# Toeplitz matrices fetched by half and copied on chip, and the experts' ends moved two steps behind their products, in a sequence mixer followed by a two-expert layer

## The chip, the cores and the metric

The kernel runs on one core of one Trainium2 chip. The metric is the device time of one execution in microseconds. Beside it stand the span and the trace of one profiled execution, from its first to its last instruction. The engines are TensorE (PE; its weight loads are PEld), VectorE (DVE), ScalarE (ACT), GpSimd (POOL) and SyncE (SP), and 16 DMA engines serve them all. SP issues ordinary transfers, POOL the indirect ones (gathers and scatters whose rows come from a table of indices).

## The reference

The input x has 2 sequences of 4096 tokens with 512 channels (8192 rows). After a layer normalisation, every channel is convolved causally with a kernel of its own, a sum of 16 decaying exponentials; and every token goes through its two best of 8 experts, 512x512 matrices, whose results are weighted and summed. The mixer's output times the silu of the experts' output is added to x.

```python
xn = _layernorm(x, axis=-1)
# mixer: q = 1 - sigmoid(delta) * sigmoid(alpha)
k = einsum('dnl,dn->dl', p * beta * exp(t * log(q)), gamma * scale)
s = irfft(rfft(xn^T) * rfft(k))[..., :l]^T + xn * omega
# experts
gate_logits = xf @ Wg.T + bg
topk_vals, topk_idx = jax.lax.top_k(gate_logits, 2)
gate_w = softmax(topk_vals)
all_out = einsum('nd,ehd->neh', xf, We) + be
g = silu(sum over the two of all_out[expert] * gate_w)
out = x + s * g
```

## The kernel before, in words

**Order of work.** All instructions of an engine are chained in the order in which the program names them (class InOrder): nothing is reordered on an engine, so an instruction that waits holds all that follow it there. Between engines only data and buffers set the order.

**Start (0 to 103 us).** 16 blocks of 4 chunks of x are loaded, normalised into `xn` (regions 0 to 3 of the buffer `big`, a quarter of the channels in each), transposed and multiplied with the gate's weights. The convolution kernels go to DRAM as `k_dram`.

**Mixer (103 to 326 us).** The 512 channels are 64 groups `g` of 8, four groups make one of 16 units `u`. A unit has products of the chunks' states (`states`, then two scans on VectorE), products with powers (`from_states`), and for each group 32 products with Toeplitz matrices (`from_chunks`), all summed in the banks `pys`; `outputs_end` copies them out, three banks by ScalarE and one by VectorE. A Toeplitz matrix of 64x64 is needed in both halves of the partitions, since `from_chunks` works with rows 0 to 63 for one half of the tokens and 64 to 127 for the other. `load_toep(g)` fetches the same 128 KB twice, once into each half of one of TB = 6 buffers, and is called five groups ahead. Between the groups the program lays other work by a table (`at(n, f, ...)`): the routing (two best experts, counting, index tables, with `val` made by POOL and consumed by TensorE), stores of the mixer's output to `s_dram` (64 of 256 KB), loads of the expert weights (16 of 512 KB, from group 33) and biases (8 of 256 KB, from group 56), and the first gathers of rows at group 58.

**Experts (326 us to the end).** The tokens are sorted by expert into NT = 71 tiles of 128 rows; round r = 0 does each token's first expert, round r = 1 its second, so `work_list` has 142 items. An item i passes through:

- `fetch(i)`: POOL gathers its rows of x (in round 1 only for the first FIRST = AHEAD + 1 tiles) and, in round 1, its rows of the mixer's output with weights and statistics from `s_dram`; AHEAD steps ahead.
- `fetch_first(i)`, in round 1: POOL gathers the first expert's result and x from `yx_dram`, which round 0 wrote.
- `mean_of(i)` (round 0) and `normalise(i)`: VectorE and a square root on ScalarE make the normalised rows, three steps ahead. `turn(i)`: TensorE transposes them and ScalarE copies them out of PSUM, two steps ahead.
- `expert(i)`: eight recorded products, whose weights are chosen by a register.
- the end, one step after: in round 0 `end_first` (VectorE adds the bias, POOL scatters into `yx_dram`); in round 1 `take_first` (ScalarE), `add_bias` and `add_expert` (VectorE, then silu on ScalarE), `put_out` (two VectorE steps, then POOL scatters to the output).

All this stands in one loop over i, whose body names the calls in a fixed order; the gathers of a step come ahead of its scatter on POOL, and the end of the earlier item comes ahead of the next `normalise` on VectorE. The products are held in a pool of 4 banks (`ps_e`), the transposes in one of 2 (`ps_t2`).

Of the kernel before, what the change touches and what calls it, by code (L numbers as in the profile page):

```python
# [8 lines left out]
FP = mybir.dt.float32  # L9
# [7 lines left out]
P = 128  # L17
EPS = 1e-5
SX = 4
IL = 2  # L20
AHEAD = 6
EARLY = 2
NOWHERE = float(1 << 20)

# [32 lines left out]
def tile_ssm_then_moe(  # L57
# [231 lines left out]
    with ExitStack() as ab:  # L289
# [33 lines left out]
        tri = abc.tile([P, P], BF)  # L323
        ones = abc.tile([P, P], BF)

        def load_toep(g):

            toep = toep_b[:, g % TB].rearrange("p h t -> p (h t)")
            src = k_dram[g * GD // IL : (g + 1) * GD // IL, 0:H]
            for h in range(2):  # L330
                io.sync.dma_start(
                    out=toep[h * H : (h + 1) * H].rearrange("p (h t) -> p h t", h=GD // IL),
                    in_=bass.AP(
                        src.tensor, src.offset, [[IL, H], [2 * H * IL, GD // IL], [1, H * IL]]
                    ),
                )
            return toep.rearrange("p (h t i) -> p h i t", i=IL, t=H)

        def powers_of(u):

# [92 lines left out]
        with ExitStack() as ph0:  # L433
# [180 lines left out]
            def gate_end(q):  # L614
                lt = ps_y.tile([P, LC, 32], FP, tag="py", name="lt")
                io.tensor.transpose(lt.rearrange("p c j -> p (c j)"), lqs_of.pop(q), ident)
                io.vector.tensor_add(
                    logits[:, q * LC : (q + 1) * LC, :], lt[:, :, 0:NE],
                    bc(gate_b.unsqueeze(1), P, LC, NE),
                )  # L620
# [61 lines left out]
                    )  # L682
            for i in range(LC):
                turn_chunk(NQ - 1, i)
            states(0, w.pop(0))
            for n in range(2):
                scan(n, decay.pop((0, n)))
# [2 lines left out]
            pys0 = banks()  # L690
            from_chunks(0, 0, pys0, toeps.pop(0))
            toeps[TB - 1] = load_toep(TB - 1)
            gate_end(NQ - 2)
            gate(NQ - 1)
            from_chunks(0, 1, pys0, toeps.pop(1))
            toeps[TB] = load_toep(TB)
            gate_end(NQ - 1)


# [251 lines left out]
        for u in range(NU):  # L951
            pys = banks() if u else pys0

            late = 0 if u else 1
            for i in range(2 * late, NS):
                g = u * NS + i
                if g + TB - 1 < G:
                    toeps[g + TB - 1] = load_toep(g + TB - 1)
                if i == 1 + late:
                    from_states(u, pys, powers.pop(u))  # L960
                    if u + 2 < NU:
                        powers[u + 2] = powers_of(u + 2)
# [12 lines left out]
                from_chunks(u, i, pys, toeps.pop(g))  # L975
                for f, args in todo:
                    if f not in first_of_group:
                        f(*args)
            outputs_end(u, sq_of(u * NS // GQ), pys)
# [4 lines left out]
    with ExitStack() as cc:  # L984
        mp = cc.enter_context(tc.tile_pool(name="more", bufs=1))
        ps_t = cc.enter_context(tc.tile_pool(name="ps_t2", bufs=2, space=PSUM))
        ps_e = cc.enter_context(tc.tile_pool(name="ps_e", bufs=4, space=PSUM))

        def more(n, width, name):
            return [mp.tile([P, width], FP, name=f"{name}{i}") for i in range(n)]  # L990

        xn_b += more(1, D, "xn")
        xnT_b += more(2, D, "xnT")
# [10 lines left out]
        for i in range(EARLY, 3):  # L1004
            mean_of(i)
            normalise(i)
            if i < 2:
                turn(i, ps_t.tile([P, KD, P], FP, name="pt"))
        held = None
        for i in range(n + 1):  # L1010
            r = work_list[i][0] if i < n else 1
            ended = work_list[i - 1][0] if i else None
            if i + AHEAD < n:
                fetch(i + AHEAD)
            if i + 3 < NT:
                mean_of(i + 3)
            if ended == 0:
                end_first(i - 1, held)
            if i == NT:
                for ii in range(NT, NT + AHEAD + 1):  # L1020
                    fetch_first(ii)
            elif i > NT and i + AHEAD < n:
                fetch_first(i + AHEAD)
            if ended == 1:
                add_expert(i - 1, held)
            if i + 3 < n:
                normalise(i + 3)
            if i + 2 < n:
                turn(i + 2, ps_t.tile([P, KD, P], FP, name="pt"))
            if i < n:  # L1030
                pe = ps_e.tile([P, D], FP, tag="pe", name="pe")
                expert(i, pe)
            if i >= NT:
                if i == NT:
                    take_first(i)
                if i < n:
                    add_bias(i)
                if i + 1 < n:
                    take_first(i + 1)
            if ended == 1:  # L1040
                put_out(i - 1)
            held = pe


# [45 lines left out]
```

## Time and profile before

| | us |
|---|---|
| median of 3 runs (943.41 to 953.67) | 945.86 |
| the profiled execution, its time | 945.91 |
| its span | 944.2 |
| busy in the span: PE / DVE / POOL / ACT | 813.7 / 583.1 / 499.4 / 365.0 |
| first expert product starts at | 325.84 |
| first gather from yx_dram starts at | 609.81 |
| last scatter starts at | 938.74 |
| DMA: 189.36 MB, of it by POOL's queue / by SP's | 126.79 MB / 61.38 MB |

A busy TensorE is not TensorE at its peak: products are pipelined and their ends are modelled. All instructions carry line 53 (a helper issues them), so they are told apart by the names of their tiles: `pe` are expert products, `pt` transposes, `py` the mixer's products, `toep_b` the Toeplitz buffers. A line of a timeline has start, duration, engine, operation, output and input tiles, and in brackets how long the engine had been idle before and what released it; a line of the chain of waits has start, duration and what the end was waiting for at that time. A line of waits has who waited for whom, total, times and longest.

### The profile page before, as it was taken

How to read it: one execution, taken by the hardware profiler on the slowest of the kernel's cores; microseconds unless marked ns; L12 is line 12 of the kernel's file. 1: busy time of each engine (PE TensorE's matmuls, PEld its weight loads, DVE VectorE, ACT ScalarE, POOL GpSimd, SP SyncE). 2: the span in 40 equal slices, each digit the busy share in tenths (PEclk: the TensorE clock that was granted, in tenths of full speed). 3: DMA queues.
4: the chain of work that ended last, by engine and by line, in shares of the span. 5: the costliest groups of instructions: out<-in, count | busy, mean ns of one | idle time of the engine just before them, and what ended most of it. 6: DMA issues, size and time to landing. Idle time of an engine off the chain costs nothing.

```text
span 944.2 us, 18704 instructions
## 1 busy us (share of the span) xinstructions
PE 813.7 (86%) x7035; PEld 482.2 (51%) x7038; DVE 583.1 (62%) x1147; ACT 365.0 (39%) x667; POOL 499.4 (53%) x480
## 2 busy tenths in 40 slices
PE   4989868887786599999999999888788996996996
PEld 3777657676675344445444444444343443443442
DVE  7786587567764255555555554185665675765685
ACT  6786645553652222222222222152332343433352
POOL 6776103220334055555555556677566675675672
PEclk9999878899997599999999999989898999997998
DMA  4667225989999995555555557588666876785771
GB/s 152 225 207 212 53 58 43 193 179 250 251 229 237 319 284 205 187 192 202 190 201 207 180 194 231 154 283 254 198 204 210 247 223 192 226 258 190 242 220 42
DMA packets 130151, 189.36 MB, mean 201 GB/s; under 512 B 19918, under 2 KB 85838, under 8 KB 130064
## 3 DMA queue, kind: packets, MB, share of 16 engines
q0 software_dynamic: 38048, 126.79, 41.0%
q1 hardware_dynamic: 92016, 61.38, 26.4%
q8 instruction: 58, 0.95, 0.4%
q14 instruction: 29, 0.24, 0.1%
HBM read 120.62 MB, written 73.01 MB: 205 GB/s over the span
## 4 chain that ended last, share of the span: by engine, by line
PE 61%; DVE 12%; issue 8%; DMA 8%; another core or an unknown queue 4%; POOL 4%; ACT 3%; SPq 1%; POOLq 0%; DVEq 0%; ACTq 0%
PE pe L53 43%; PE pt L53 7%; PE py L53 5%; DVE big L53 4%; DVE came_b L53 3%; PE ph L53 2%; DMA big<-in_x_rev 2%; ACT big L53 2%; DVE st L53 1%; PE lq L53 1%; DMA toep_b<-k_dram 1%; DMA big<-in_b_e 1%; POOL big L53 1%; DMA big<-yx_dram,x_idx 1%
## 5 line engine op out<-in xcount | busy, mean ns | idle before, releaser
L53 PE MATMUL pe<-big 128*128 x576 | 265.2, 604 | 0.8 <-DMA big<-in_w_e 0.8
L53 PE MATMUL pe<-big,xnT 128*128 x560 | 258.3, 605 | 0.0
L53 PEld LDWEIGHTS pe<-big 128*128 128x128 f32 x576 | 106.7, 195 | 109.2 <-issue 109.2
L53 PEld LDWEIGHTS pe<-big,xnT 128*128 128x128 f32 x560 | 103.6, 195 | 104.7 <-issue 104.7
L53 ACT ACTIVATE big<-big 128x512 f32<-128x512 f32 x103 | 66.6, 651 | 186.0 <-DVE big L53 117.9
L53 PEld LDWEIGHTS pt<-ident,big 128*128 128x128 f32 x636 | 88.9, 190 | 89.8 <-issue 78.4
L53 PE MATMUL pt<-ident,big 128*128 128x128 f32 x636 | 103.8, 301 | 34.8 <-DVE big L53 20.1
L53 POOL TENSOR_TENSOR val<-hot,token 128x568 bf16<-128x568 bf16 x32 | 38.9, 1214 | 157.5 <-DVE hot L53 130.6
L53 ACT COPY big<-pt 128x512 f32<-128x512 f32 x136 | 76.6, 593 | 99.3 <-PE pt L53 84.3
L53 PE MATMUL py<-big,toep_b 64*64 64x64 f32 x2048 | 88.5, 242 | 27.3 <-DMA toep_b<-k_dram 10.6
L53 POOL DMA_INDIRECT out<-big,o_idx x71 | 75.3, 1061 | 68.9 <-DVE big L53 49.7
L53 PEld LDWEIGHTS py<-big,toep_b 64*64 64x64 f32 x2048 | 77.8, 152 | 38.7 <-issue 14.5
L53 POOL DMA_INDIRECT yx_dram<-big,o_idx x47 | 57.9, 1231 | 72.1 <-DVE sm L53 68.0
L53 DVE TENSOR_TENSOR big<-pe,big 128x512 f32<-128x512 f32 x47 | 32.5, 691 | 88.3 <-PE pe L53 81.3
L53 ACT COPY xnT<-pt 128x512 f32<-128x512 f32 x70 | 40.5, 578 | 83.1 <-PE pt L53 73.4
L53 POOL TENSOR_SCALAR big<-big,stats 128x512 f32<-128x512 f32 x44 | 55.9, 1347 | 23.1 <-ACT stats L53 10.1
L53 DVE SCALAR_TENSOR_TENSOR big<-pe,sg,big 128x512 f32<-128x512 f32 x42 | 31.5, 750 | 53.1 <-PE pe L53 28.3
L53 POOL DMA_INDIRECT big<-in_x,x_idx x52 | 51.2, 984 | 20.2 <-issue 16.3
L53 ACT ACTIVATE sm<-sm,eps 128x1 f32<-128x1 f32 x71 | 20.9, 294 | 86.2 <-DVE sm L53 86.2
L53 POOL DMA_INDIRECT sg<-s_dram,x_idx x42 | 46.4, 1104 | 12.8 <-issue 9.8
L53 DVE TENSOR_TENSOR big<-big 128x512 f32<-128x512 f32 x73 | 50.3, 689 | 3.4 <-ACT big L53 1.9
L53 POOL DMA_INDIRECT big<-yx_dram,x_idx x44 | 44.3, 1007 | 14.9 <-issue 12.8
(152 smaller groups left out, 1089.2 us busy)
## 6 DMA issues: line engine op xcount, KB each, us to landing
big<-in_x_rev SPq DMA_DIRECT2D x16, 1024.0 KB
toep_b<-k_dram SPq DMA_DIRECT2D x128, 128.0 KB
s_dram<-big SPq DMA_DIRECT2D x64, 256.0 KB
big<-in_w_e SPq DMA_DIRECT2D x16, 512.0 KB
big<-in_b_e SPq DMA_DIRECT2D x8, 256.0 KB
out<-big,o_idx POOLq DMA_INDIRECT x71
big<-in_x,x_idx POOLq DMA_INDIRECT x52
yx_dram<-big,o_idx POOLq DMA_INDIRECT x47
```

What stands on the lines that cost most here:

```text
L53: return lambda *args, **kwargs: self.order.follow(make(*args, **kwargs))
```

## The change

First, `load_toep(g)` fetches one half only (rows 0 to 63 for even g, 64 to 127 for odd), and `double_toep(g)` copies it to the other half: ScalarE for groups with g % 4 of 0 or 2, POOL for the others. The copy stands two groups ahead of its use, after `from_chunks` of group g - 2.

Second, in the experts' loop the end of an item comes BEHIND = 2 steps after its product (1 at the very end), rows are made ready up to READY = 5 steps ahead and turned three ahead, AHEAD is 7 (so FIRST is 8), and the pools grow: `ps_e` has 6 banks, `xn` 4 buffers for 3, `xnT` 5 for 4, `x_b` 8 for 7. At the boundary of the rounds three gathers from `yx_dram` are named at once and the other five singly, one a step beside the regular one, where all seven stood together.

```diff
+DOUBLED = 2
+TO_ACT = (0, 2)
-AHEAD = 6
+AHEAD = 7
+READY = 5
+TURNED = 3
+BEHIND = 2
...
+        def toep_of(g, half):
+            return toep_b[half * H : (half + 1) * H, g % TB].rearrange("p h t -> p (h t)")
...
         def load_toep(g):
-            toep = toep_b[:, g % TB].rearrange("p h t -> p (h t)")
             src = k_dram[g * GD // IL : (g + 1) * GD // IL, 0:H]
-            for h in range(2):
-                io.sync.dma_start(
-                    out=toep[h * H : (h + 1) * H].rearrange("p (h t) -> p h t", h=GD // IL),
...
+            io.sync.dma_start(
+                out=toep_of(g, g % 2).rearrange("p (h t) -> p h t", h=GD // IL),
...
+        def double_toep(g):
+            copy = io.scalar.copy if g % NS in TO_ACT else io.gpsimd.tensor_copy
+            copy(toep_of(g, 1 - g % 2), toep_of(g, g % 2))
...
                 from_chunks(u, i, pys, toeps.pop(g))
+                if g + DOUBLED < G:
+                    double_toep(g + DOUBLED)
...
-        ps_e = cc.enter_context(tc.tile_pool(name="ps_e", bufs=4, space=PSUM))
+        ps_e = cc.enter_context(tc.tile_pool(name="ps_e", bufs=6, space=PSUM))
...
-            if i + 3 < NT:
-                mean_of(i + 3)
-            if ended == 0:
-                end_first(i - 1, held)
...
+            to_be = i + 3 + min((i + 1) // 2, READY - 3)
+            make_ready(to_be, True)
+            ends = range(ended, i - (BEHIND if i < n - 2 else 1) + 1)
+            ended = max(ended, ends.stop)
+            for e in ends:
+                if e < NT:
+                    end_first(e, held.pop(e))
+                elif e == ends[0]:
+                    add_expert(e, held.pop(e))
+            if ended >= NT:
+                for ii in late[: 3 if len(late) > AHEAD else 1]:
+                    late.remove(ii)
                     fetch_first(ii)
-            elif i > NT and i + AHEAD < n:
-                fetch_first(i + AHEAD)
...
+                if i + AHEAD < n:
+                    fetch_first(i + AHEAD)
+            make_ready(to_be, False)
+            for ii in range(turned, min(i + 2 + (i >= 4), n - 1) + 1):
+                turn(ii, ps_t.tile([P, KD, P], FP, name="pt"))
+                turned = ii + 1
             if i < n:
-                pe = ps_e.tile([P, D], FP, tag="pe", name="pe")
-                expert(i, pe)
...
+                held[i] = ps_e.tile([P, D], FP, tag="pe", name="pe")
+                expert(i, held[i])
+            if ended == NT and ends:
+                take_first(NT)
+                add_bias(NT)
+                take_first(NT + 1)
+            for e in ends:
+                if e >= NT:
+                    if e > ends[0]:
+                        add_expert(e, held.pop(e))
+                    if e + 1 < n:
+                        add_bias(e + 1)
+                    if e + 2 < n:
+                        take_first(e + 2)
+                    put_out(e)
```

More of the change, by code (lines that the diff above doesn't have):

```diff
@@ L324, in tile_ssm_then_moe @@
         ones = abc.tile([P, P], BF)
+        def toep_of(g, half):
+            return toep_b[half * H : (half + 1) * H, g % TB].rearrange("p h t -> p (h t)")
         def load_toep(g):
-            toep = toep_b[:, g % TB].rearrange("p h t -> p (h t)")
             src = k_dram[g * GD // IL : (g + 1) * GD // IL, 0:H]
-            for h in range(2):
-                io.sync.dma_start(
-                    out=toep[h * H : (h + 1) * H].rearrange("p (h t) -> p h t", h=GD // IL),
[L333 to L337, printed above, removed]
+            io.sync.dma_start(
+                out=toep_of(g, g % 2).rearrange("p (h t) -> p h t", h=GD // IL),
+                in_=bass.AP(
+                    src.tensor, src.offset, [[IL, H], [2 * H * IL, GD // IL], [1, H * IL]]
+                ),
+            )
+            return toep_b[:, g % TB].rearrange("p h t -> p (h t)").rearrange(
+                "p (h t i) -> p h i t", i=IL, t=H
+            )
+        def double_toep(g):
+            copy = io.scalar.copy if g % NS in TO_ACT else io.gpsimd.tensor_copy
+            copy(toep_of(g, 1 - g % 2), toep_of(g, g % 2))
         def powers_of(u):
@@ L684, in tile_ssm_then_moe @@
                 turn_chunk(NQ - 1, i)
+            for g in range(DOUBLED):
+                double_toep(g)
             states(0, w.pop(0))
@@ L692, in tile_ssm_then_moe @@
             toeps[TB - 1] = load_toep(TB - 1)
+            double_toep(DOUBLED)
             gate_end(NQ - 2)
@@ L696, in tile_ssm_then_moe @@
             toeps[TB] = load_toep(TB)
+            double_toep(DOUBLED + 1)
             gate_end(NQ - 1)
@@ L986, in tile_ssm_then_moe @@
         ps_t = cc.enter_context(tc.tile_pool(name="ps_t2", bufs=2, space=PSUM))
-        ps_e = cc.enter_context(tc.tile_pool(name="ps_e", bufs=4, space=PSUM))
+        ps_e = cc.enter_context(tc.tile_pool(name="ps_e", bufs=6, space=PSUM))
         def more(n, width, name):
             return [mp.tile([P, width], FP, name=f"{name}{i}") for i in range(n)]
-        xn_b += more(1, D, "xn")
-        xnT_b += more(2, D, "xnT")
+        xn_b += more(2, D, "xn")
+        xnT_b += more(3, D, "xnT")
         yx_b += more(4, 2 * D, "yx")
@@ L1003, in tile_ssm_then_moe, with make_ready @@
             fetch(i)
[L1004 to L1009, printed above, removed]
+        ready, turned, ended, held = EARLY, EARLY, 0, {}
+        def make_ready(upto, before_ends):
+            nonlocal ready
+            for i in range(ready, min(upto, n - 1) + 1):
+                if before_ends:
+                    if i < NT:
+                        mean_of(i)
+                else:
+                    normalise(i)
+                    ready = i + 1
@@ L1010, in tile_ssm_then_moe @@
+        late = list(range(NT, NT + AHEAD + 1))
+        for before_ends in (True, False):
+            make_ready(2, before_ends)
         for i in range(n + 1):
-            r = work_list[i][0] if i < n else 1
-            ended = work_list[i - 1][0] if i else None
             if i + AHEAD < n:
                 fetch(i + AHEAD)
-            if i + 3 < NT:
-                mean_of(i + 3)
-            if ended == 0:
-                end_first(i - 1, held)
-            if i == NT:
-                for ii in range(NT, NT + AHEAD + 1):
-                    fetch_first(ii)
-            elif i > NT and i + AHEAD < n:
-                fetch_first(i + AHEAD)
@@ L1024, in tile_ssm_then_moe @@
[L1024 to L1029, printed above, removed]
-            if i < n:
-                pe = ps_e.tile([P, D], FP, tag="pe", name="pe")
-                expert(i, pe)
[L1033 to L1039, printed above, removed]
@@ L1040, in tile_ssm_then_moe @@
-            if ended == 1:
-                put_out(i - 1)
-            held = pe
+            to_be = i + 3 + min((i + 1) // 2, READY - 3)
[10 more added lines that the diff above has]
+                    late.remove(ii)
+                    fetch_first(ii)
+                if i + AHEAD < n:
+                    fetch_first(i + AHEAD)
```

## The prediction

> **What bounds the kernel now.** I read the table by stage first, then the chain of waits around each place where TensorE loses busy time, then the timelines of POOL, VectorE and TensorE there.
>
> ```profile
> core 0: us, PE busy (x) PEld busy (x) DVE busy (x) ACT busy (x) POOL busy (x), PEclk, DMA share, GB/s
> 165.00:215.00 50.00, 40.81 (x1119) 34.80 (x1116) 29.57 (x45) 26.82 (x52) 11.77 (x11) 0.88 0.89 188
> 215.00:265.00 50.00, 39.54 (x1097) 34.00 (x1097) 36.23 (x64) 25.90 (x49) 9.71 (x8) 0.90 0.99 249
> 265.00:306.00 41.00, 29.24 (x788) 24.87 (x784) 24.50 (x40) 15.90 (x25) 17.00 (x15) 0.88 1.06 230
> 306.00:326.00 20.00, 8.02 (x77) 6.60 (x78) 5.73 (x15) 5.07 (x9) 0.95 (x1) 0.50 1.03 339
> 326.00:590.00 264.00, 264.00 (x810) 130.04 (x811) 139.92 (x335) 58.42 (x134) 150.93 (x137) 0.99 0.61 207
> 618.00:936.00 318.00, 280.82 (x818) 135.38 (x816) 217.94 (x345) 120.63 (x208) 210.98 (x199) 0.95 0.69 218
> ```
>
> Three regimes are seen. From 165 to 326 us (the sequence mixer) the DMA engines are full (share 0.89 to 1.06). From 326 to 590 us (the first round of experts) TensorE is busy all the time, 3.873 us for an item. From 618 to 936 us (the second round) no engine is full: 318 us for what would be 275 us (71 x 3.873).
>
> ```profile
> 293.39 5.44 DMA toep_b<-k_dram
> ...
> 305.22 10.78 DMA big<-in_b_e
> ...
> 316.01 9.59 DMA big<-in_w_e
> ...
> 325.84 6.00 PE pe L53 x8
> 314.72 0.47 PE L53 MATMUL py<-big,toep_b 64*64 64x64 f32 x2 [5.13 <-DMA toep_b<-k_dram]
> ```
>
> The end of the mixer hangs on transfers: the last Toeplitz groups, then biases and expert weights that queue behind them. The first expert product starts at 325.84 us.
>
> ```profile
> 658.51 0.98 POOL L53 DMA_INDIRECT yx<-yx_dram,x_idx  x1 [0.30 <-issue]
> 659.79 1.01 POOL L53 DMA_INDIRECT out<-big,o_idx  x1 [0.30 <-issue]
> 661.11 0.98 POOL L53 DMA_INDIRECT sg<-s_dram,x_idx  x1 [0.30 <-issue]
> 662.39 0.95 POOL L53 DMA_INDIRECT big<-yx_dram,x_idx  x1 [0.30 <-issue]
> 669.57 1.01 POOL L53 DMA_INDIRECT out<-big,o_idx  x1 [6.23 <-DVE big L53]
> 666.10 0.75 DVE L53 SCALAR_TENSOR_TENSOR big<-pe,big 128x512 f32<-128x512 f32 x1 [7.44 <-remote]
> 667.45 1.09 PE L53 MATMUL pt<-ident,big 128*128 128x128 f32 x4 [6.58 <-DVE big L53]
> DVE big L53 <- remote: 42.5, 8, 10.3
> ```
>
> The last line is from the waits of 618 to 936 us. VectorE stops for 5 to 10 us some eight times, TensorE then waits for rows that VectorE has not made, and POOL for a row to put out. But POOL is nearly full as well: each item costs it two gathers and a scatter. From 609.81 to 904.16 us I count 190 POOL starts; waits over the usual 0.3 us gap add up to 35.9 us, and the rest is 1.367 us a DMA, so 4.10 us an item when nothing holds it, against TensorE's 3.873. In the second round TensorE is not the resource to watch; POOL is.
>
> **What the Trainium skill says.** "Runtime: NRT & Kernel Launch", section Instruction fetch mechanics: each engine streams its program in blocks over its own DMA queue, the crossing mostly hidden. The page's own table has two instruction queues (58 packets, 0.95 MB; 29 packets, 0.24 MB, thus 8.3 KB each). VectorE's stops at 650, 718, 784 and 845 us are 61 to 68 us apart, some 16 or 17 items, so I read the "remote" stops as such fetches; in the first round all but one are hidden, in the second they are not. That the fetch is the cause is inferred. "DMA: Bandwidth & Descriptors", section Queues, rings and completion order: every DMA engine goes round-robin over the queues, a packet at a time; a fetch or a weight load then waits beside whatever else is queued. This fits, but no line shows it alone. "ScalarE: Activation LUTs", section What ACT_TABLE_LOAD costs: 186 ns + 0.833 ns an element with immediate operands, thus 613 ns for 512; the trace has 578 and 593 ns for its 128x512 copies.
>
> **Part 1: Toeplitz halves.** Removed: 64 of the 128 DMAs toep_b<-k_dram, 128 KB and 256 pieces of 512 bytes each. Price of a piece: in 165-215 us, 0.89 x 50 us x 16 engines = 712 us of engine time moved 9.4 MB, nearly all in 512-byte pieces, 18,400 of them: 39 ns. Some 41 of the removed DMAs lie after 165 us: 41 x 256 x 39 ns / 16 = 25.6 us of a stretch that is full from 165 to 326 us. That is the DMA side's bound: the weights could land by about 301 us. On SP 64 issues of 0.59 us go too, ahead of the stores, weights and biases in its order, and with them waits for earlier transfers.
>
> Then TensorE is late next. It ended group 61 at 302.1 us. Left are two groups at 1.97 us, eight transposes at 1.97 together and the transposes of one more item at 1.09: 309 us. Ahead of that stand 3.15 us in which TensorE waited for POOL's val, itself behind a gather that waited for stores (2.33 us), and 13.6 us of "issue" gaps between 165 and 300 us, where between 103 and 165 us (DMA share 0.38) there was under 1. Emptier queues should give back some; bounds 0 and 12 us, I take 4. So the first expert product starts at 305: 21 us earlier, bounds 12 and 26.
>
> Added: 32 copies of 64x512 on ScalarE at 0.58 (18.6 us in a stage where it is busy about half) and 32 on POOL. No such POOL copy is in the trace; its one-input TENSOR_SCALAR of 128x512 takes 1.35 us, which I take; a plain copy may be down at 0.8. That is 43 us on an engine with 46 us of work in 165-306 us. Both are issued two groups (some 6 us) ahead of use, so nothing of them is on TensorE's path unless the transfer is late. The new wait: a copy holds ScalarE or POOL until its half has landed. Behind it on ScalarE are the powers, the decays, w and the copies of py that free the banks; on POOL val and the first gathers. The load is issued five groups ahead and the copy waits for it after three, so about 9 us of lead where the products had 15. Only the last two groups overran 15 us before, with SP ten microseconds behind; with the queue relieved I cost it at 0, upper bound 5 us (included in the 12 above).
>
> **Part 2: experts.** First round: TensorE remains full, 3.873 us an item; end two steps later and rows earlier change only what waits beside it. Its 71 items are 275 us as before.
>
> Boundary: the second round's first gather from yx_dram has to wait for the last scatter of the first. Before, POOL had two gathers (1.29 + 1.26 us) ahead of that scatter; now FIRST is 8 and only one is left, and a part of its lag goes: first gather about 2.3 us earlier relative to TensorE. TensorE stood 6.0 us there; with rows turned three ahead it can run four items past the boundary, so that stall goes, but POOL sets the pace from here.
>
> Second round, POOL: from the first yx_dram gather to the last are 194 starts, 193 x 1.367 = 264 us plus waits. Of the 35.9 us of waits, about 14 follow TensorE's own short stops (at 693, 752, 818, 892 us): with TensorE up to three items ahead these are hidden. The VectorE stops remain, since add_expert, put_out and so the scatter all stand behind them. How much of a stop POOL can cover is set by a loop: scatter, two gathers, landing, normalise, add_bias, the two steps of put_out, next scatter. I measure it at one place: scatter at 640.00, yx_dram gather at 642.77, landed 647.67, output row done at 650.30: 10.3 us. Before, the loop spanned four items (4 x 4.10 = 16.4, so POOL could lag 6 us, and did: 5.6 us at 655.90). Now AHEAD is 7, but rows are taken five ahead and ended two behind: three items, 12.3 us, so a lag of 2.0 us only. Stops of 5.15, 7.4, 6.0, 6.0 and 10.3 us less 2 each are 25 us. Waits 36 to 25: 11 us gained. From the last gather to the end were 28.6 us (915.61 to 944.2), and I leave them.
>
> **Sum.** 21 + 2.3 + 11 = 34.3 us: span 909.9, and with 1.7 us around it (945.91 against 944.2) 911.6 us. The profiled execution is 0.05 us from the median of 945.86, so no shift.
>
> **Rivals.**
> 1. The stops are absorbed wholly, and only POOL's own work is left in round two: 609.8 - 23.3 = 586.5, + 264 + 28.6 = 879, so 881 us. For it: TensorE gets a cover of some 11 us. Against: every output row passes VectorE, then POOL, which cannot catch up at 4.10.
> 2. Stage one gains, but POOL waits as long as before in round two: 944.2 - 23.3, so 922.6 us. For it: the shorter loop; against: TensorE's stops were a third of its waits.
> 3. The mixer doesn't gain, because copies held by late transfers cost what the fewer bytes bring: 944.2 - 13.3, so 932.6 us. Against it: share 1.06 just where it ends.
> 4. Slower: the three-item loop. If a yx_dram gather takes longer than 4.9 us to land, the loop grows past 12.3 us and paces the round. There are some 20 trips (61 scatters / 3); each microsecond over 6.9 costs 20 us, so from 8.6 us of landing the whole gain is gone, and at 9.3 us the time is 911.6 + 48 = 960 us. For it: two transfers more are asked for early, and POOL idles less. Against: 4.3 to 5.2 us wherever the trace lets it be read, at a DMA share of 0.69.
>
> **How the numbers follow.** Forecast 911.6 us: 0.42. Rival 1: 0.16; rival 2: 0.18; rival 3: 0.12; rival 4: 0.12. The range of 882 to 937 takes in rival 1 to rival 3 and leaves out rival 4 and a little at the fast end. A measurement of this kernel tells about 1% from no change. Faster by over 1% (below 936.4): the forecast, rivals 1 and 2 and a quarter of rival 3, which ends near that bound: 0.79. Within 1%: 0.1. Slower: 0.11.
>
> **What would show it.** First expert product near 305 us, and no wait for toep_b in TensorE's last groups; ScalarE and POOL copies of toep_b without long waits for DMA. In the second round, POOL starts 1.37 us apart with waits of about 25 us, VectorE's remote stops still there, TensorE's waits at most short and spread. I am wrong if the first expert product starts after 315 us, if VectorE waits for yx_dram gathers at most steps (rival 4), or if POOL's spacing falls well under 1.36.

## The result, and the profile after

The changed kernel took 937.17 us (median of 17 runs, 930.88 to 942.35), the kernel before 946.03 us beside it (17 runs, 937.91 to 955.5): ratio 0.9908, 95% interval 0.9884 to 0.9931. It is faster by 0.9%, where 3.6% were forecast. The profiled execution has a span of 935.5 us, 8.7 less than before.

Two things have to be known for the numbers below. First, later sets of runs fell on different chips, and these are of two kinds: the kernel before takes some 947 us on some and some 900 us on others. Each set has the kernel before beside it, and ratios are taken within one set alone. Each of these chips was met in one set only, so a chip and its occasion cannot be told apart; "kind of chip" stands for both. Second, on chips of the second kind the kernel before falls into two groups (in one set 11 of 43 runs at 883 to 891 us, the others at 894 to 913), and the ratios rest mostly on the lower one, so there they stand above what the medians say.

The table by stage, with the columns of before:

```profile
core 0: us, PE busy (x) PEld busy (x) DVE busy (x) ACT busy (x) POOL busy (x), PEclk, DMA share, GB/s
165.00:215.00 50.00, 40.65 (x1148) 34.67 (x1145) 34.92 (x48) 35.27 (x67) 19.39 (x21) 0.95 0.70 168
215.00:265.00 50.00, 40.63 (x1183) 35.12 (x1189) 39.93 (x69) 34.11 (x61) 17.80 (x18) 0.95 0.87 220
265.00:306.00 41.00, 28.32 (x687) 24.16 (x673) 21.02 (x38) 14.50 (x24) 18.83 (x19) 0.83 1.00 285
326.00:590.00 264.00, 264.00 (x823) 130.50 (x822) 153.05 (x320) 51.77 (x130) 142.10 (x143) 1.00 0.59 205
618.00:936.00 318.00, 266.46 (x759) 126.93 (x757) 212.92 (x331) 114.21 (x196) 205.27 (x190) 0.93 0.64 206
```

The DMA engines did become emptier between 165 and 265 us (0.89 and 0.99 before), but TensorE's busy time there is the same as before within 1.1 us. Where the mixer ends, TensorE's timeline has:

```profile
294.71 0.63 PE L58 MATMUL tab<-val,at 128*128 128x142 bf16 x4 [6.30 <-POOL val L58]
295.27 3.68 PE L58 MATMUL py<-big,toep_b 64*64 64x64 f32 x58
310.83 1.09 PE L58 MATMUL pt<-ident,xn 128*128 128x128 f32 x4 [4.54 <-DVE xn L58]
312.64 1.19 PE L58 MATMUL pe<-big 128*128 x1 [0.73 <-DMA s_dram<-big]
```

and POOL's:

```profile
285.20 0.95 POOL L58 DMA_INDIRECT big<-in_x,x_idx  x1 [0.30 <-issue]
292.83 0.61 POOL L58 COPY toep_b<-toep_b 64x512 f32<-64x512 f32 x1 [6.69 <-DMA toep_b<-k_dram]
293.53 1.13 POOL L58 TENSOR_TENSOR val<-hot,token 128x568 bf16<-128x568 bf16 x1
```

TensorE's last long waits for a Toeplitz transfer are gone (5.13 us at 314.72 before). The same kind of late transfer now holds POOL's copy for 6.69 us, `val` stands behind the copy, and TensorE waits 6.30 us for `val`. The first expert product starts at 312.64 us instead of 325.84.

The second round, from TensorE's, VectorE's, ScalarE's and POOL's timelines around one stop, and from the table of waits of 618 to 936 us ("remote" stands where the signal that ended a wait has no instruction that ended shortly before it):

```profile
629.74 3.60 PE L58 MATMUL pe<-big 128*128 x8
636.11 0.63 PE L58 MATMUL pt<-ident,big 128*128 128x128 f32 x4 [2.77 <-ACT xnT L58]
636.57 5.29 PE L58 MATMUL pe<-big 128*128 x8
641.71 0.60 PE L58 MATMUL pt<-ident,big 128*128 128x128 f32 x4
642.14 3.60 PE L58 MATMUL pe<-big,xnT 128*128 x8
653.43 1.11 PE L58 MATMUL pt<-ident,xn 128*128 128x128 f32 x4 [7.69 <-ACT xnT L58]
...
651.33 0.75 DVE L58 SCALAR_TENSOR_TENSOR big<-pe,sg,big 128x512 f32<-128x512 f32 x1 [6.05 <-remote]
652.79 0.59 ACT L58 COPY xnT<-pt 128x512 f32<-128x512 f32 x1 [9.86 <-remote]
656.39 1.02 POOL L58 DMA_INDIRECT out<-big,o_idx  x1 [5.88 <-DVE big L58]
...
ACT xnT L58 <- remote: 47.1, 8, 9.9
PE pt L58 <- ACT xnT L58: 28.4, 7, 7.7
DVE big L58 <- remote: 23.0, 7, 6.4
```

VectorE and ScalarE stop together and go on within 1.5 us of each other. What each waits for is TensorE's: VectorE a product (`pe`), ScalarE a transposed row (`pt`). Counted item by item, the product that VectorE reads at 651.33 us is the one that ended at 633.34, and the row that ScalarE copies at 652.79 the one that was transposed by 636.74. TensorE's records go on meanwhile, to 645.74, through two more products; only then does TensorE wait itself, for ScalarE. The trace's record of semaphore signals agrees: TensorE's five signals for what ended from 633.34 to 645.74 stand at 651.31, 652.77, 652.87, 652.92 and 653.02 us. The last two products among these ended 3.9 us apart and were signalled 0.15 us apart. So "remote" here is not a stop of VectorE's own: TensorE's completions reach the others late, and in a bunch, while its records show the work itself as done. Before, VectorE showed most of these stops (42.5 us, ScalarE 10.0), since it ended each item one step after its product; now ScalarE, which serves rows three ahead, shows most of them.

POOL's starts from the first yx_dram gather to the last, counted as before the change: 194 instead of 198, 1.387 us each instead of 1.370, waits of 34.7 us instead of 35.9.

### The profile page after: what moved, and what is told of

It reads as the page before. It is cut to its first block, busy times and chain, and to the rows that moved or that the text cites. A ratio compares the mean times of both kernels' runs of the same rounds, so it can differ in the third digit from the quotient of the medians.

```text
span 935.5 us, 18673 instructions
## 1 busy us (share of the span) xinstructions
PE 813.0 (87%) x7035; PEld 479.3 (51%) x7038; DVE 608.4 (65%) x1147; ACT 379.2 (41%) x699; POOL 511.9 (55%) x513
## 4 chain that ended last, share of the span: by engine, by line
PE 39%; issue 16%; DVE 14%; POOL 13%; ACT 8%; DMA 6%; another core or an unknown queue 4%; POOLq 0%; SPq 0%; DVEq 0%; ACTq 0%
PE pe L58 26%; PE pt L58 5%; ACT big L58 5%; DVE big L58 4%; POOL big L58 4%; DVE came_b L58 4%; PE py L58 4%; POOL out L58 3%; DMA toep_b<-k_dram 2%; PE ph L58 2%; DMA big<-yx_dram,x_idx 2%; POOL sg L58 2%; POOL yx_dram L58 1%; POOL yx L58 1%
## 5 line engine op out<-in xcount | busy, mean ns | idle before, releaser
L58 PE MATMUL pe<-big,xnT 128*128 x672 | 311.7, 608 | 0.0
L58 PE MATMUL pe<-big 128*128 x464 | 214.6, 607 | 0.7 <-DMA s_dram<-big 0.7
L58 PEld LDWEIGHTS pe<-big,xnT 128*128 128x128 f32 x672 | 125.0, 196 | 127.2 <-issue 127.2
L58 PEld LDWEIGHTS pe<-big 128*128 128x128 f32 x464 | 86.0, 195 | 89.2 <-issue 88.9
L58 PEld LDWEIGHTS pt<-ident,big 128*128 128x128 f32 x544 | 75.5, 198 | 69.8 <-issue 38.1
L58 PE MATMUL pt<-ident,big 128*128 128x128 f32 x544 | 87.5, 299 | 27.1 <-ACT xnT L58 13.5
L58 POOL DMA_INDIRECT yx_dram<-big,o_idx x47 | 47.8, 1017 | 74.2 <-DVE big L58 72.4
L58 PEld LDWEIGHTS pt<-ident,xn 128*128 128x128 f32 x280 | 35.4, 145 | 63.1 <-issue 43.0
L58 PE MATMUL pt<-ident,xn 128*128 128x128 f32 x280 | 44.1, 282 | 24.7 <-ACT xnT L58 14.9
L58 POOL COPY toep_b<-toep_b 64x512 f32<-64x512 f32 x32 | 23.6, 743 | 53.8 <-DMA toep_b<-k_dram 52.4
```

Of the source, the lines that this page charges most:

```text
L58: return lambda *args, **kwargs: self.order.follow(make(*args, **kwargs))
```

## Experiments

"Waits of POOL" are its gaps over 0.31 us between the first and the last yx_dram gather; "to the end" is from the first yx_dram gather to the end of POOL's last scatter, some 5 us before the span's end (329.9 us before, 333.2 after).

**Set 1** (the kernel before 947.16 us, 11 runs; 6 runs each).

*Toeplitz part alone* (e1) and, below, *experts' part alone* (e2): one file's mixer joined to the other's experts' loop.

```diff
-AHEAD = 7
+AHEAD = 6
...
-        ps_e = cc.enter_context(tc.tile_pool(name="ps_e", bufs=6, space=PSUM))
+        ps_e = cc.enter_context(tc.tile_pool(name="ps_e", bufs=4, space=PSUM))
...
```

These are lines of e1 against the changed kernel (`...` stands for lines left out); e2 has the same lines the other way round against the kernel before.

> Only the Toeplitz part of the change; the experts' loop, AHEAD and the buffers are those of the kernel before. Theory A (the mixer gives all of the gain, since the second round's stops are TensorE's late completions, which no cover on VectorE's side removes): first expert product near 313 us as with the whole change, second round as before, so about 937 us, ratio 0.990. Rival B (the experts' part costs what the Toeplitz part wins): about 922 us, ratio 0.975. Rival C (the Toeplitz part gives nothing, the earlier start of the mixer was chance and the experts' part gives the 0.9%): 946 us, ratio 1.00.

942.47 us, ratio 0.9987 (0.9938 to 1.0035). First expert product at 317.08 us.

> Only the experts' part; the Toeplitz halves are both fetched as before. Theory A: first expert product near 326 us, POOL's waits in the second round 33 to 37 us as before, time 944 to 947 us, ratio 1.00. Rival B: 955 to 962 us, ratio 1.01 to 1.02. Rival C: 937 us, ratio 0.990.

945.57 us, ratio 1.0005 (0.9958 to 1.0051). First product at 325.93, waits of POOL 26.0 us, to the end 323.8. Neither part alone can be told from no change here. B is excluded by both, C in this set by e2, and A's 0.990 for e1 is missed too: at the first expert product the profile of e1 is 8.9 us ahead of that of e2, which has the old fetch; at the end e1's median is 4.7 us below that of the kernel before. That POOL's waits were 26.0 in one execution and about 35 in others shows how far one profile carries.

*All copies on ScalarE* (e3):

```diff
-TO_ACT = (0, 2)
+TO_ACT = (0, 1, 2, 3)
```

> The whole change, but all 64 copies of Toeplitz halves on ScalarE, none on POOL. Theory A (POOL was held 52.4 us by copies whose half had not landed, and val behind one of them cost TensorE 6.30 us near the end of the mixer): TensorE's wait for val goes back to about 3 us or less, first expert product 308 to 310 us, time about 933 us, ratio 0.986. Rival D (whichever engine copies is held by the same late transfers): ScalarE is held instead, powers, decays and the copies that free banks wait behind it, first expert product 313 to 318 us, time 937 to 943 us, ratio 0.991 to 0.997.

938.16 us, ratio 0.9926 (0.9882 to 0.997), first product at 315.48 us: rival D. TensorE's longest wait from 98 us to its first expert product is

```profile
PE py L58 <- ACT toep_b L58: 13.5, 9, 4.9
```

TensorE waits 0.8 us for `val` (14.2 with the change), but the products now wait 13.5 us for ScalarE's copies (6.2 us with the change). So POOL's copies did cause the waits for `val`, and moving them moved the wait.

*Copies one group ahead* (e4):

```diff
-DOUBLED = 2
+DOUBLED = 1
```

> The whole change, but each Toeplitz half copied one group ahead of its products instead of two (DOUBLED = 1), so that a transfer has four groups of lead before a copy waits for it. Theory A: POOL's 52.4 us of waits for toep_b halve, the 6.30 us wait for val shrinks to 3 us, first expert product 308 to 310 us, ratio 0.986. Rival D (the transfers are late for the products themselves, so TensorE waits for the copy in place of val): first expert product 313 to 317 us, TensorE's own waits for toep_b 10 us or more, ratio 0.991 to 0.996.

969.10 us, ratio 1.0243 (1.0188 to 1.0299); first product at 343.00 us, 28 to 30 us later than with two groups ahead. TensorE's waits in that stage:

```profile
PE py L58 <- ACT toep_b L58: 40.1, 14, 6.4
PE py L58 <- POOL toep_b L58: 5.1, 1, 5.1
```

Theory A fell. POOL's waits for toep_b transfers shrank only from 52.4 to 42.6 us. ScalarE had no wait for a transfer ahead of its copies, and yet they came too late 14 times. The reason left is their place: a copy, 0.6 us long, also has to get its turn between powers, decays and bank copies. A place in ScalarE's order thus has a price even where the transfer is in time; the prediction had set it at 0.

**Set 2** (the kernel before 896.56 us, 31 runs): the other kind of chip. None of its four profiles shows a remote stop in the second round.

*Half the product in the second round* (f1), *no gate rows after the tenth item* (f2), *rows four ahead* (f3), *one expert* (f4), the edits abridged:

```diff
 f1, in expert:     nk = KD // 2 if r else KD;  for k in range(nk)
 f2, in fetch:      if r == 1 and j < 10: gather(sg_b...)
 f3:                READY = 4
 f4, in experts_of: if r == 1: return 0
```

> The whole change, but in the second round each expert product sums only two of its four chunks of 128, so that TensorE has some 2.2 us of work an item instead of 3.87 (the output rows lack half of their product). Theory A (TensorE, nearly as full as POOL and late again after every idle stretch, is what VectorE and ScalarE wait for in the 'remote' stops): the stops go, POOL's waits in the second round fall from 35 to under 8 us, first to last yx_dram gather from 302 to about 275 us, time about 910 us, ratio 0.96. Rival E (the three-item loop of gather, normalise, end and scatter paces the round, TensorE only sits in it): POOL still waits 25 to 35 us, time 930 to 937 us. Rival F (the stops belong to the fetch of instructions, whatever the work): 8 or 9 stops stay, time 925 to 935 us.

> The whole change, but in the second round only the first ten items fetch their gate row (sg<-s_dram); later items use a row left in the buffer, so that POOL has two DMAs an item instead of three. Theory A (POOL's starts are the second round's bound, with TensorE just below): the round runs at TensorE's 3.87 us an item or its stops, first to last yx_dram gather 275 to 285 us instead of 302, time 912 to 920 us, ratio 0.965 to 0.975. Rival E (a loop of latencies paces the round): no change beyond 1%, 930 to 940 us.

> The whole change, but rows made ready four items ahead instead of five (READY = 4), so that the loop of gather, normalise, end and scatter spans four items again instead of three. Theory A: the stops come from TensorE, so no change beyond 0.5%: 933 to 941 us, POOL's waits 30 to 38 us. Rival E (the three-item loop took back what two more items of cover gave): POOL's waits fall to 20 us or less, VectorE's waits for yx_dram gathers (14.7 us between 618 and 936 us) go, time 918 to 925 us, ratio 0.97 to 0.98.

> The whole change, but in the second round every item takes the weights and the bias of expert 0, whose place is fixed, so that TensorE and VectorE load no indices into registers and compute no addresses; TensorE's program is 24 instead of 30 instructions an item. Theory A: the stops do not depend on it, time within 0.5% of the whole change, 933 to 941 us. Rival F (register loads or instruction fetches hold TensorE): stops gone or a fifth rarer (one in 10 to 11 items instead of one in 8 to 9), POOL's waits under 25 us, time 915 to 927 us.

f1 896.54 us (ratio 1.0108, 1.0041 to 1.0175), f2 877.23 (0.9866, 0.9792 to 0.9939), f3 893.39 (1.0037, 1.0006 to 1.0068), f4 896.59 (1.009, 1.0052 to 1.0128). Waits of POOL were 2.7 us in f1, 1.8 in f3, 2.7 in f4, and to the end 297 us in all three. With the stops absent everywhere, f1 and f4 say nothing on the stops' cause, and f3 nothing on what the loop of three items costs where there are stops. f1 shows that TensorE is not the bound without stops: with half of its products the stretch from the first to the last yx_dram gather is no shorter (268.2 us, and 267.5 with all of them on a like chip, set 5). f2 is clear: with two POOL DMAs an item, that stretch falls to 238.2 us and POOL waits 56 us (the columns are those of the table by stage):

```profile
592.00:830.00 238.00, 238.00 (x740) 117.50 (x739) 206.05 (x308) 108.28 (x187) 141.10 (x132) 1.00 0.66 218
```

Now TensorE is busy in all of it. So without stops POOL's starts bound the second round, with TensorE next.

**Set 3** (949.01 us, 49 runs; the first kind of chip).

> The kernel before, unchanged, for its profile on the chip that runs the next three (the chips of the two sets so far differ: in the first set the kernel before took 947 us with some nine stops of TensorE in the second round, in the second set 897 us and the variants there showed none). Theory A (the stops belong to the chip): where this set's granted clock stays at 1.00 in the second round there are no remote stops, POOL's waits are under 6 us and the time is 885 to 900 us; where the clock falls to half in pieces, eight or nine stops, waits of 26 to 46 us, 940 to 950 us. Rival G (the stops belong to the kernel before and go with the edits of the second set): stops and 36 us of POOL waits on any chip.

> The whole change, unchanged, beside the three others of this set. Theory A: without stops the second round is POOL's 193 starts at 1.387 us = 268 us with waits under 4 us, mixer 9 to 12 us shorter than before; POOL's starts before the last yx_dram gather are 4 fewer and 2 output rows more follow it, so the experts' part gives nothing and the whole is the mixer's 9 to 12 us, ratio 0.987 to 0.990. Rival H (without stops the longer cover costs its two items at the end): ratio 0.995 to 1.005.

> The Toeplitz part alone again. Theory A: the same as the whole change within 0.3%: mixer 9 to 12 us shorter, ratio 0.987 to 0.990. Rival H: better than the whole change by 0.5 to 1.0%.

> The experts' part alone again. Theory A: ratio 0.997 to 1.003, POOL's waits in the second round no smaller than before. Rival H: ratio 1.005 to 1.012, with last yx_dram gather to the end 5 us longer and nothing gained ahead of it.

A copy of the kernel before: 947.41 us, ratio 0.9936 (0.9905 to 0.9968), although it is the same code; differences below 0.6% are therefore not told apart by these ratios. The 0.9908 of the result stands 0.3% beyond that, and comes again here. The whole change: 938.39, 0.9888 (0.9844 to 0.9933), inside theory A's 0.987 to 0.990. Toeplitz part: 943.70, 0.9951 (0.9914 to 0.9988), short of it. Experts' part: 940.39, 0.9928 (0.989 to 0.9966), where theory A had 0.997 to 1.003 and rival H over 1.005: both missed. The whole change is 9 and 11 us faster in the two sets on such chips that have it; by the medians the Toeplitz part has 5 of these and the experts' part 2 to 9, no sharper.

The copy of before has stops again, 47.4 us on VectorE between 618 and 830 us, so rival G fell: they came and went with the chip, not with the edits. ScalarE's timeline of the whole change in this set:

```profile
649.84 0.58 ACT L58 COPY xnT<-pt 128x512 f32<-128x512 f32 x1 [9.34 <-remote]
688.46 0.58 ACT L58 COPY big<-pt 128x512 f32<-128x512 f32 x1 [9.95 <-remote]
728.60 0.58 ACT L58 COPY xnT<-pt 128x512 f32<-128x512 f32 x1 [9.67 <-remote]
766.56 0.58 ACT L58 COPY xnT<-pt 128x512 f32<-128x512 f32 x1 [8.77 <-remote]
805.12 0.58 ACT L58 COPY big<-pt 128x512 f32<-128x512 f32 x1 [8.95 <-remote]
```

and VectorE's of the Toeplitz part alone (set 1), where AHEAD is 6:

```profile
789.34 0.75 DVE L55 SCALAR_TENSOR_TENSOR big<-pe,sg,big 128x512 f32<-128x512 f32 x1 [7.58 <-remote]
823.52 0.75 DVE L55 SCALAR_TENSOR_TENSOR big<-pe,sg,big 128x512 f32<-128x512 f32 x1 [7.67 <-remote]
857.70 0.75 DVE L55 SCALAR_TENSOR_TENSOR big<-pe,big 128x512 f32<-128x512 f32 x1 [7.70 <-remote]
```

The distances are 38.0 to 40.1 us here and 34.2 there. Eight items of POOL's 4.1 us and a wait of 5.5 us (a figure that was chosen to fit; POOL's wait in the stop shown above was 5.88) make 38.3; seven and the same wait make 34.2. Eight and seven are AHEAD + 1: a stop holds the gathers of the items AHEAD ahead, and may come back when these reach TensorE. That is a guess from two regular profiles. Others do not show it: in the first profile of the kernel before, AHEAD 6 as well, VectorE's six stops of over 3 us end 10.7 to 66.3 us apart.

**Set 4** (899.87 us, 36 runs; again the second kind).

*Half the product in the second round* (h1, as f1), *in the first round only* (h2), *rows scattered two steps later* (h3), *no gate rows* (h4, as f2), the edits abridged:

```diff
 h2, in expert:   nk = KD if r else KD // 2
 h3, in put_out:  to_go.append((r, j, o))
                  if len(to_go) > LAG: scatter(out, *to_go.pop(0))
```

> As in the second set: half of each product's chunks left out in the second round (the output rows lack that half), on a chip with the stops if this is one. Theory A (the stops are TensorE's, by its load): no or short stops, POOL's waits under 8 us, first yx_dram gather to the end 297 to 300 us instead of 333, ratio 0.95 to 0.96. Rival E (a loop of latencies or the boundary's burst starts the stops, whatever TensorE's load): POOL's waits 25 to 40 us, 325 to 335 us from the first gather to the end, ratio 0.985 to 0.995.

> Half of each product's chunks left out in the first round only; the second round is whole. Theory A (what counts is the load of the stage itself): the first round shortens to POOL's or VectorE's pace, the second keeps eight or nine stops and 325 to 335 us from the first yx_dram gather to the end. Rival J (the stops are the price of 264 us in which TensorE was never idle, a limit with a memory): few stops in the first 100 us of the second round, POOL's waits 20 us or less, 305 to 320 us from the first gather to the end.

> The whole change, with each output row scattered two steps after it was made (LAG = 2, one more output buffer, one xn buffer less), so that POOL's gathers do not stand behind a late row; the cover of a stop grows by some 8 us. Theory A (with its stops TensorE, 275 us of work and some 45 us of stops, is the bound of the second round): POOL waits elsewhere instead (for buffers or rows), first yx_dram gather to the end 328 to 338 us, ratio 0.985 to 0.995. Rival K (POOL is the bound, and its waits behind a late row are what the stops cost): POOL's waits under 12 us, 305 to 312 us from the first gather to the end, ratio 0.96 to 0.97.

> As in the second set: from the eleventh item on the second round fetches no gate row and uses one left in the buffer. Theory A (TensorE with its stops is the bound on a chip that shows them): first yx_dram gather to the end 320 to 333 us, against 274 us on the chip without stops. Rival K (POOL is the bound in either case): 300 to 310 us.

h1 898.37 us (1.0063, 1.0031 to 1.0095), h2 845.41 (0.9441, 0.9348 to 0.9534), h3 894.90 (1.0021, 0.9985 to 1.0058), h4 880.00 (0.9847, 0.9761 to 0.9932). With its three xn buffers h3 takes, for items 5 and 6 of the first round, the rows of items 8 and 9. No stop came in any of the four, so none could do what it was made for. Waits of POOL: 3.3, 2.7, 1.6 us; h4 58. One thing is shown: in h1 TensorE's granted clock goes to half in pieces of 3.4 to 6.8 us, 0.92 on average from 618 to 864 us, and no stop goes with it.

```profile
618.00:864.00 246.00, 156.30 (x467) 68.83 (x467) 186.32 (x292) 101.21 (x177) 191.39 (x177) 0.92 0.81 250
```

So the half clock went here with a TensorE that was busy for 156.30 of 246 us (in set 5, at 236.92 of 246, the clock was 1.00), and it does not by itself make the stops.

**Set 5** (902.51 us, 43 runs; the second kind): the whole change (i1), and the later scatter with the buffers of the change (i2).

> The whole change, unchanged. On a chip where the kernel before takes some 947 us, theory A: ratio 0.987 to 0.991 once more, 13 or more remote stops, 331 to 335 us from the first yx_dram gather to the end. On a chip where the kernel before takes some 897 us, theory A: no stops, POOL's waits under 4 us, 297 us from the first gather to the end, 890 to 898 us, so within 1% of before; rival H (there the whole gain of the mixer is kept): ratio 0.985 to 0.990.

> The whole change with each output row scattered two steps after it was made (LAG = 2; buffers as in the change). On a chip with stops, theory A (TensorE with its stops is the bound): ratio to the kernel before as for the whole change within 0.4%. Rival K (POOL's waits behind a late row are the price of the stops): POOL's waits under 12 us, 305 to 315 us from the first gather to the end, ratio 0.965 to 0.975. On a chip without stops both: as the whole change within 0.3%.

i1: 898.36 us, ratio 1.008 (1.0044 to 1.0117). i2: 893.61, ratio 1.0035 (1.0001 to 1.007). By the ratio the change is 0.8% slower here than the kernel before, by the medians 0.5% faster: a gain is not shown on this kind of chip. i1's table by stage has the second round as

```profile
618.00:864.00 246.00, 236.92 (x705) 109.10 (x704) 187.19 (x293) 102.31 (x178) 191.17 (x179) 1.00 0.82 253
```

The lines of i2's edit are those of h3, without the change of buffers. In i1: granted clock 1.00, no remote stop, waits of POOL 2.0 us, first to last gather 267.5 us. The later scatter gives 0.5% over the change on this chip, with waits of 0.9 us; rivals A and K part only where stops are, and there it has not run. Against the kernel before it is not shown to be faster.

## Why the prediction was wrong, point by point

The four terms of the sum in the profiled pair, forecast and measured: first expert product 21 and 13.2 us earlier; from there to the first yx_dram gather 2.3 gained and 0.7 lost (283.97 to 284.66); first to last yx_dram gather 11 and 3.4 gained (305.80 to 302.40); from there to the end 0 and 7.2 lost (28.6 to 35.8). Sum 34.3 and 8.7: the 25.6 us that are missing are 7.8, 3.0, 7.6 and 7.2, so no single term carries the miss. One entry was inconsistent with the prediction's own figures: 264 us of starts and 25 of waits are 289, which is 16.8 less than the 305.80 of before, and it entered 11.

**The mixer: the direction right, the size wrong.** The pair's 13.2 us flatter the change. Over four profiles with the old fetch (325.84, 320.30, 325.93, 321.81) and four with the copies on the same kind of chip (312.64, 315.41, 317.08, 316.04) the first expert product comes 8.2 us earlier on average, and 2.4 of these lie in the start stage, which ended 102.3 and 99.9 us after the span's start. The step that failed is "the DMA side's bound" with TensorE late next at 309 us: 25.6 us of DMA time less were taken to leave only TensorE's own work in the way, so that the mixer would end 21 us earlier. The DMA time was removed, but TensorE had not been waiting for all of it. TensorE's table of waits of before, 102 to 326 us, which the prediction did not read, has what it did wait for:

```profile
PE py L53 <- DMA toep_b<-k_dram: 10.6, 4, 5.1
PE tab L53 <- POOL val L53: 7.9, 7, 3.1
```

After, from 98 to 313 us:

```profile
PE tab L58 <- POOL val L58: 14.2, 8, 6.3
PE py L58 <- ACT toep_b L58: 6.2, 2, 3.8
PE tab L58 <- POOL toep_b L58: 1.1, 1, 1.1
PE py L58 <- DMA toep_b<-k_dram: 0.3, 1, 0.3
```

10.3 us of waits for transfers went, and 13.6 us came with the copies (6.3 more for `val`, 6.2 and 1.1 for copies). What remained as a gain came from shorter waits elsewhere ("issue" 4.8 us less, for VectorE 4.5, for ScalarE's rows 1.5) and from the earlier start. The other profiles agree: in all four with the old fetch TensorE waits 7.0 to 10.6 us for Toeplitz transfers and 7.2 to 8.0 for `val`, in all four with the copies 0.3 and 12.4 to 16.7. That emptier DMA queues shortened the waits elsewhere is likely, but not shown. The cost "0, upper bound 5 us" of a held copy was the second error, with 13.6 us measured: e3 moved it to the other engine, and e4 raised TensorE's waits for copies to 45 us; neither removed it. POOL's copy itself was cheaper than assumed, 0.743 us on average against 1.35 (the 0.8 that the prediction held possible rested on no trace). Of the cases that were laid out, rival 3 (copies held by late transfers cost what fewer bytes bring) is the nearest, in number; it too counted on the second round's gain.

**The boundary.** The order of POOL's gathers changed as described, but the 2.3 us did not come: the stretch took 283.5 to 284.4 us in the four profiles with the old loop and 283.9 to 285.7 in the six with the new one, on chips with stops. There the stops begin late in the first round (after: VectorE went on at 572.8 us after 4.6, ScalarE at 591.7 after 8.9; before: VectorE at 594.2 after 5.4), so they may have hidden a gain. Where there were no stops, this stretch took 280.2 us in i1 and 281.6 in f3; the old loop has no profile there.

**The second round: POOL as the bound, right; the stops, wrong.** f2 and h4 show the bound, on chips without stops. There the count of the prediction holds within 3.5 us: rival 1's 264 us for POOL's own work against 267.5 in i1. The step that read VectorE's stops as its instruction fetches failed, and the trace of before could have told: of VectorE's six stops of over 3 us in the second round (5.15, 7.44, 6.06, 6.06, 3.71 and 10.29 us) none overlaps the transfer of a block on either instruction queue, and the 61 to 68 us between stops left out two of the six. (The two instruction queues with 58 and 29 packets that the prediction names are those of the profile of before, not of a page of the Trainium skill.) The same program has the stops on one kind of chip (in the profile after 47.1 us for one group of ScalarE's copies and 23.0 on VectorE) and none on the other, with the same number of blocks; and what ScalarE and VectorE wait for is TensorE.

With that the term "25 us of waits" fell too. On the first kind of chip POOL waited 35.9, 46.6, 29.8 and 43.8 us in the four profiles with the old loop (before, e1, g1, g3), on average 39.0, and 34.7, 26.0, 34.5, 35.6, 39.6 and 34.7 in the six with the new one (after, e2, e3, e4, g2, g4), on average 34.2. From the first yx_dram gather to the span's end the averages are 339.6 and 336.2 us, with ranges that overlap (331.8 to 347.8, 328.3 to 338.6). So a gain of 3 to 5 us is possible, not 11, and these profiles do not prove it. A cover on VectorE's side leaves TensorE's late signals where they are; the stops moved from VectorE to ScalarE.

**The tail.** Four starts fewer ahead of the last gather (5.5 us) and two output rows more after it (10 instead of 8, 7.2 us): the work was moved behind the last gather. The prediction left the tail as it was. Part of the 7.2 is chance of the pair: on average of the same four and six profiles the tail grew from 31.3 to 34.4 us.

**Rival 4** (the loop of three items slows the round) did not come where there are no stops: with READY at 5 as at 4, POOL waits 2 to 3 us there. Where there are stops it is untested. VectorE's waits for yx_dram gathers rose there from 1.9 us before to 35.6 after (618 to 936 us), though POOL's waits did not, so the shorter loop may have cost a part of what the cover gave.

**Open.** What makes TensorE's signals late on some chips stays open. Whether its load in the second round or the full 264 us of the first matters is not known (h1 and h2 were to tell, and fell on chips without stops). A rival that no run tests is the recording itself: in all ten profiles with stops some semaphore signals are missing (VectorE has 1092 signalling instructions and 898 to 961 recorded signals), in the ten without stops none are; and no run without the recording is on record. Nor is it known why the mixer's gain does not show in the ratios on chips without stops, for which there is no profile of the kernel before.

## What to carry to other kernels

A DMA share near 1 prices nothing by itself. Read first the consumer's own wait for those transfers in that stage (10.6 us here, not 25.6); relief elsewhere can come on top (some 11 us of TensorE's other waits here), but it has to be found in the trace too. A copy that replaces a transfer is bought with a place in an in-order engine, and it is held by the transfer that it copies; whatever stands behind it there inherits the wait. When a wait is put down to something unknown, look which other engines resume close to it and what all of them wait for, count which piece of work each of them gets, and lay the supposed cause beside every stop, not only those that fit, before giving it a name.

## What the runs showed of the hardware

The same program differs by 5% from one kind of chip to the other (some 947 and some 900 us), nearly all of it in the second round: with the change, from the first yx_dram gather to the end, 333.2 us against 296.4, where the whole times are 937.2 and 898.4.

On the slower kind TensorE's signals can come long after the work that they report: at 651.33 us VectorE got a product that TensorE's records end at 633.34, and four signals came within 0.25 us. TensorE's granted clock in i1 stays at 1.00 in the second round, against 0.93 after the change where the stops are; in h1 it was 0.92 without a stop.

With nothing to hold it, POOL started an indirect DMA every 1.376 us (i1, 193 starts in 265.5 us); with two instead of three an item the stretch fell from 267.5 to 238.2 us. POOL copies a half of 64x512 floats in 0.61 to 1.57 us (median 0.612, mean 0.743).
